# Softplus stages on a time line of the scan's half steps, in a four-layer hybrid kernel

## The chip, the core and the metric

The kernel runs on one NeuronCore of a Trainium2 chip. A core has TensorE (matmuls, into the memory PSUM), VectorE (elementwise work, reductions, scans), ScalarE (activation functions), GpSimd (here elementwise work, called POOL in the profile), and SyncE, whose queue (SP) issues nearly all DMAs. Each engine takes its own instructions strictly in the program's order; semaphores order them between engines. The metric is the device time of one launch in microseconds (us), lower is better.

## The reference

Four layers work on four images of 32 x 32 x 256. Layer 0 has a depthwise convolution and a state-space scan with 64 states for each of 512 channels, layer 1 a grouped convolution, layer 2 a masked attention and eight experts, layer 3 a scan with 16 states and eight experts. The change touches the step sizes of the two scans. In layer 0:

```python
proj = x @ w_x
dt_raw, Bm, Cm = jnp.split(proj, [R, R + N], axis=-1)
dt = jax.nn.softplus(dt_raw @ w_dt + dt_bias)
A = -jnp.exp(A_log)
def step(h, inp):
    xt, dtt, Bt, Ct = inp
    dA = jnp.exp(dtt[:, :, None] * A)
    h = dA * h + (dtt * xt)[:, :, None] * Bt[:, None, :]
    y = jnp.einsum('bdn,bn->bd', h, Ct)
    return (h, y)
```

and in layer 3 in the same way `dt = softplus(x_conv @ W_dt + b_dt)`, with a matrix of 512 x 512.

## The kernel before, in words

**The backbone.** `scans` runs eight scans one after the other, in the order (0,0), (0,1), (3,0), (0,2), (3,1), (0,3), (3,2), (3,3) of (layer, image): 256 units each for layer 0 and 64 for layer 3, 1280 in all. A unit is 128 rows of (state, channel) by 1024 time steps. A DMA loads dt, spread over the rows, into a tile `dA` (five buffers); ScalarE makes the exponential of it in place, in pairs of units; TensorE spreads dt*x to the rows (`ps_rep`, from the bf16 parts `S`, two buffers); VectorE multiplies by B and then runs the scan; GpSimd multiplies the result h by C; TensorE collects the rows (`ps_y`). The generator stops (`yield`) twice a unit, once after the multiply and once after the scan is issued: a half unit.

**The side chain.** All other work is one chain of stages (`STAGES`), issued between the half units: `front` 0 to 3 (layer 0 up to the step sizes of the image), `middle` b (the rest of layer 0 and all of layers 1 and 2, then `front3`, layer 3 up to the step sizes), `last` b (the rest of layer 3). A stage may start when its scan is done, or far enough. The scan of a later image needs the step sizes from a stage; `need` forces the chain on where they are not there in time. The last 64 units, (3,3), begin after `middle` 3; while the chain is at that, no scan is left to run beside it.

**How much of the chain goes between two half units.** `run` keeps a planned clock for each engine (`Metered`, fed with rough costs in us as instructions are issued). After each half unit it lifts every clock to at least 4 us (`LAG`) behind VectorE's, and then calls `advance`, which runs the chain to its next `yield`, up to twice (`TICKS`), as long as no clock is ahead of VectorE's:

```python
for e in clock:
    clock[e] = max(clock[e], now - LAG)
for _ in range(TICKS):
    if max(clock.values()) > clock["vector"] + LEAD or self.advance() is None:
        break
```

These clocks set the order of the program; nothing of them is known at run time.

**The softplus stage.** `steps` makes dt and dt*x of one image in eight items (d, g): four blocks of 128 channels by two halves of 512 time steps. For an item, `project` is the product in PSUM (`ps_dt`; one matmul in layer 0, four in layer 3), Relu to `r` and Abs to `e` on ScalarE (`linear`), then a load of the table for Exp and Ln, Exp, Identity with bias 1 and Ln to `l` (`soft`). `add` is one operation on VectorE (reads the PSUM tile) and three on GpSimd: dt ends up in `r`, dt*x in `l`. `split` issues the store of dt to DRAM (SP), casts dt*x to bf16 on ScalarE, has VectorE subtract that (`sp_x`), and casts the rest on ScalarE: the two upper of three bf16 parts. `low` makes the third on GpSimd, `store` issues the store of the three parts. Buffers: `r` and `l` three, `e` two, the parts three. `pipe` runs five steps as a software pipeline: one tick holds `store`, `low`, `split`, `add` and `project` of five items in sequence, the oldest first, and yields once.

For the last scan, (3,3), the first two items are done ahead of the rest, in another order (`between`), and `beside` puts a tick of another generator, the experts of image 2, behind each tick of this stage.

Of the kernel before, what the change touches and what calls it, by code (L numbers as in the profile page):

```python
# [31 lines left out]
SCANS = ((0, 0), (0, 1), (3, 0), (0, 2), (3, 1), (0, 3), (3, 2), (3, 3))  # L32
# [9 lines left out]
SCATTERED = 1  # L42
AHEAD = 12
LATEST = 5
DRAIN = 4
BETWEEN = 8

# [2 lines left out]
LEAD, LAG, TICKS = 0.0, 4.0, 2  # L50
# [87 lines left out]


END = object()  # L140


class Hybrid:
# [56 lines left out]
    def pipe(self, items, *steps, cost=1.0, cut=False):  # L200


        items = list(items)
        for tick in range(len(items) + len(steps) - 1):
            for s in reversed(range(len(steps))):
                if 0 <= tick - s < len(items):
                    steps[s](items[tick - s])
                    if cut and s:
                        yield cost
            yield cost if tick < len(items) else 0.5  # L210
# [173 lines left out]
    def scans(self, mp, psum):  # L384
# [15 lines left out]
        final = next(k for k, unit in enumerate(units) if unit[0] == SCANS[-1])  # L400
        units[final:final] = [None] * DRAIN
        final += DRAIN
        chunks, rows, waiting = {}, {}, []
# [60 lines left out]
        def chunks_ahead(k, late=False):  # L464
# [5 lines left out]
            while waiting:  # L470
                scan, d = units[waiting[0]][:2]
                if ("parts", *scan, d) not in self.ready:
                    if waiting[0] - k > (1 if waiting[0] == final else LATEST):
                        break
# [145 lines left out]
    def run(self):  # L620

        self.done, self.ready = set(), set()
        self.todo, self.stage, self.wait = list(STAGES), None, None
        self.alone, self.reached, self.passed = False, 0, set()
        nc, tc = self.nc, self.tc
        with tc.tile_pool(name="scan", bufs=1) as mp, tc.tile_pool(
            name="scps", bufs=1, space=PSUM
        ) as psum, tc.tile_pool(name="sdps", bufs=1, space=PSUM) as side, tc.manual_schedule():
            self.side_psum(side)
            self.scan_psum = psum  # L630
            self.mask_work, self.sorted = self.setup(), False
            clock = self.clock = dict.fromkeys(Metered.COST, 0.0)
            self.nc = Metered(nc, clock)
            for n, _ in enumerate(self.scans(mp, psum)):
                now = clock["vector"]
                if n % 2 and clock["gpsimd"] < now:
                    next(self.mask_work, None)
                for e in clock:
                    clock[e] = max(clock[e], now - LAG)
                for _ in range(TICKS):  # L640
                    if max(clock.values()) > clock["vector"] + LEAD or self.advance() is None:
                        break
            while self.advance() is not None:
                pass
            self.nc = nc
        assert not self.todo

    def steps(self, fp, key, w, src, chunks, bias, u, between=None):  # L650


        nc = self.nc
        for d in range(DC):
            self.keep(("dt", *key, d), [P, L])
            self.keep(("parts", *key, d), [3, P, L], BF16)
        got = {}

        def tile2(tag, bufs):
            return fp.tile([P, 512], F32, tag="sp_" + tag, name="sp_" + tag, bufs=bufs)  # L660

        def linear(item):
            d, g = item
            ps = self.ps("ps_dt")
            self.mm(ps, lambda k: w(k, d), src, chunks, slice(g * 512, (g + 1) * 512))

            r, e, l = (tile2(t, n) for t, n in (("r", 3), ("e", 2), ("l", 3)))
            nc.scalar.activation(r, ps, AF.Relu, bias=bias[:, d : d + 1])
            nc.scalar.activation(e, ps, AF.Abs, bias=bias[:, d : d + 1])
            got[item] = r, e, ps, l  # L670

        def soft(item):
            _, e, ps, l = got[item]
            nc.scalar.activation(e, e, AF.Exp, scale=-1.0)
            nc.scalar.activation(ps, e, AF.Identity, bias=1.0)
            nc.scalar.activation(l, ps, AF.Ln)

        def project(item):
            linear(item)
            self.log_table()  # L680
            soft(item)

        def add(item, by=nc.gpsimd):
            d, g = item
            r, e, one, l = got[item]
            nc.vector.scalar_tensor_tensor(e, one, -1.0, e, ALU.add, ALU.subtract)
            by.tensor_tensor(l, l, e, ALU.subtract)
            by.tensor_tensor(r, l, r, ALU.add)
            by.tensor_tensor(l, r, u[:, d, g * 512 : (g + 1) * 512], ALU.mult)

        def split(item):
            d, g = item
            r, _, _, x = got[item]
            nc.sync.dma_start(self.mem["dt", *key, d][:, g * 512 : (g + 1) * 512], r)
            X = fp.tile([P, 3, 512], BF16, tag="parts", name="parts", bufs=3)
            rest = tile2("x", 2)
            nc.scalar.copy(X[:, 0, :], x)
            nc.vector.tensor_tensor(rest, x, X[:, 0, :], ALU.subtract)
            nc.scalar.copy(X[:, 1, :], rest)
            got[item] = rest, X  # L700

        def low(item, by=nc.gpsimd):
            rest, X = got[item]
            by.tensor_tensor(X[:, 2, :], rest, X[:, 1, :], ALU.subtract)

        def store(item):
            d, g = item
            _, X = got.pop(item)
            nc.sync.dma_start(
                self.mem["parts", *key, d][:, :, g * 512 : (g + 1) * 512].rearrange("s p t -> p s t"), X  # L710
            )
            if g == 1:
                self.ready.add(("parts", *key, d))

        items = [(d, g) for d in range(DC) for g in range(2)]
        if between is not None:
            ahead, items = items[:2], items[2:]
            for item in ahead:
                linear(item)
            self.log_table()  # L720
            for item in ahead:
                soft(item)
            yield from between
            self.begin(key)
            for item in ahead:
                add(item, nc.vector)
            for item in ahead:
                split(item)
            self.two_loads()
            for item in ahead:  # L730
                low(item, nc.vector)
            self.first_parts = [got.pop(item)[1] for item in ahead]
            self.parts_direct(range(1), nc.scalar)
            self.ready.add(("parts", *key, 0))
            yield 3.0
        yield from self.pipe(items, project, add, split, low, store, cost=3.0)

# [871 lines left out]
    def moe(self, which, b, tb, side="right", pause=False):  # L1611
# [8 lines left out]
        with ExitStack() as stack:  # L1620
# [8 lines left out]
            def begin():  # L1629
                nonlocal op  # L1630
                op = stack.enter_context(tc.tile_pool(name=f"m{which}{b}", bufs=1, side=side))
                weights[0] = expert_weights(0)
# [68 lines left out]
            if pause:  # L1701
                yield END
                begin()
# [367 lines left out]
    def beside(self, main, other, begin=lambda: True):  # L2071

        held = None
        for cost in main:
# [3 lines left out]
            held = None  # L2078
            more = next(other, END)
            if more is END:  # L2080
                other = None
# [8 lines left out]
    def rest(self, other):  # L2090
        for more in other or ():
            if more is END:
                return
            yield more
# [14 lines left out]
    def last(self, b):  # L2109
# [4 lines left out]
        if b == NB - 1:  # L2114
            for more in self.other:
                if more is not END:
                    yield more
# [50 lines left out]
```

## Time and profile before

| | us |
|---|---|
| median of 3 runs (6305.61 to 6317.68) | 6310.74 |
| the profiled execution | 6294.21 |
| its span, from first to last instruction | 6292.5 |
| VectorE busy | 5032.7 (80%) |
| TensorE busy (matmuls) | 5142.7 (82%) |
| GpSimd busy | 3825.9 (61%) |
| ScalarE busy | 3410.6 (54%) |

The profile is one execution on the chip. In its lines an instruction is named by engine, operation and tiles, "out<-in"; buffer numbers are left out. `x` before a number is a count. A line of a group has the busy time, the mean in ns of one instruction, then the idle time of the engine just before the group's instructions and what ended most of it. A line of waits has the total of a kind, how often, and the longest. A line of windows has the stretch in us from the span's start and its length, then the busy time of each engine in it, the share of its full clock that TensorE was granted, the share of DMA time and GB/s. All source lines are L131, the helper that counts the planned clocks, so groups are told apart by their tiles: `sp_r`, `sp_e`, `sp_l`, `sp_x`, `parts` and `ps_dt` are the softplus stage's.

When softplus stages run (first activation to the end of the last third part), and how many scan units were started before each:

| scan | us | units |
|---|---|---|
| (0,0) | 94 to 216 | 0 to 19 |
| (0,1) | 409 to 515 | 61 to 84 |
| (0,2) | 695 to 792 | 127 to 147 |
| (0,3) | 956 to 1058 | 189 to 210 |
| (3,0) | 2006 to 2108 | 443 to 463 |
| (3,1) | 3064 to 3167 | 699 to 719 |
| (3,2) | 4433 to 4535 | 1027 to 1047 |
| (3,3) | 5647 to 5779 | 1216 to 1234 |

### The profile page before, as it was taken

To read this page: it belongs to the slowest core of one execution; us is meant where nothing else is said; L and a number is where in the kernel's file an instruction comes from. 1 tells how busy PE (TensorE), PEld (TensorE's weight loads), DVE (VectorE), ACT (ScalarE), POOL (GpSimd) and SP (SyncE) were. 2 spreads that over 40 slices of the span, in tenths; PEclk is the share of its full clock that TensorE was granted. 3 is DMA by queue.
4 is the path that set the end of the run, shared out by engine and by line. 5 is a ranking of instruction groups with operands and counts; after the bars stand their busy time and mean duration, and the time that the engine had idled before them with its cause. 6 is when DMAs were issued, how large, how long until landed. Compare 5 with 4: busy or idle time off the path is not lost. (4 is left out here: it accounts for less than half of the span.)

```text
span 6292.5 us, 59823 instructions
## 1 busy us (share of the span) xinstructions
PE 5142.7 (82%) x20249; PEld 2117.1 (34%) x20249; DVE 5032.7 (80%) x4016; ACT 3410.6 (54%) x4299; POOL 3825.9 (61%) x1948
## 2 busy tenths in 40 slices
PE   5676785579798568979869969989689779997999
PEld 2122120132253122234225522244145332543566
DVE  5888898988898998889889988899889982317811
ACT  3565655345496435558638735567547544336621
POOL 2787768665586766568767756577867752006600
PEclk7687785589798668979969979979779889999989
DMA  3555555544355656445455576345545761027611
GB/s 109 160 158 167 165 175 185 159 150 136 113 173 177 194 165 170 132 128 191 159 178 174 182 179 165 119 150 195 174 156 179 208 161 48 19 73 184 166 34 34
DMA packets 347915, 934.97 MB, mean 149 GB/s; under 512 B 37748, under 2 KB 120256, under 8 KB 345984
## 3 DMA queue, kind: packets, MB, share of 16 engines
q1 hardware_dynamic: 344880, 928.38, 48.7%
q0 software_dynamic: 2128, 2.13, 0.2%
q8 instruction: 165, 2.70, 0.2%
q14 instruction: 166, 1.36, 0.1%
q10 hardware_dynamic: 576, 0.39, 0.0%
HBM read 841.02 MB, written 92.37 MB: 148 GB/s over the span
## 5 line engine op out<-in xcount | busy, mean ns | idle before, releaser
L131 POOL TENSOR_TENSOR h<-h,rows 128x1024 f32<-128x1024 f32 x1280 | 3024.2, 2366 | 1740.4 <-DVE h L131 1529.3
L131 DVE TENSOR_TENSOR_SCAN h<-dA,ps_rep 128x1024 f32<-128x1024 f32 x1280 | 2924.3, 2285 | 182.2 <-ACT dA L131 53.6
L131 DVE TENSOR_TENSOR ps_rep<-ps_rep,rows 128x1024 f32<-128x1024 f32 x1280 | 1549.4, 1210 | 142.6 <-PE ps_rep L131 141.7
L131 PE MATMUL ps_rep<-S,spread_L_conv_A_log 96*128 96x512 bf16 x2048 | 752.8, 456 | 770.3 <-DVE h L131 722.4
L131 ACT ACTIVATE dA<-dA,A_L_conv_A_log 128x1024 f32<-128x1024 f32 x1024 | 1125.4, 1142 | 440.0 <-DMA dA<-dt 405.7
L131 PE MATMUL ps_y<-h,collect_L_conv_A_log 128*32 128x512 f32 x4096 | 704.4, 741 | 15.3 <-POOL h L131 15.3
L131 PE MATMUL ps_e<-we,h_m 128*128 128x256 f32 x3072 | 709.4, 383 | 8.3 <-ACT h_m L131 8.3
L131 PEld LDWEIGHTS <-spread_L_conv_A_log 96*128 96x128 bf16 x2048 | 159.7, 102 | 1558.0 <-DVE h L131 1246.4
L131 PEld LDWEIGHTS ps_e<-we,h_m 128*128 128x128 f32 x3072 | 583.3, 191 | 159.2 <-ACT h_m L131 31.0
L131 PE MATMUL ps_h<-xTm,we 128*128 128x512 f32 x1280 | 603.3, 607 | 4.6 <-DMA we<-in_L_ffn_W_dram 4.5
L131 ACT ACT_TABLE_LOAD x402 | 515.8, 1283 | 37.0 <-PE ps_h L131 15.5
L131 ACT ACTIVATE h_m<-ps_h,cols 128x512 f32<-128x512 f32 x384 | 257.5, 686 | 423.0 <-PE ps_h L131 421.0
L131 ACT ACTIVATE p<-ps_sc 128x512 f32<-128x512 f32 x404 | 219.3, 594 | 316.7 <-PE ps_sc L131 306.1
L131 ACT ACTIVATE dA<-dA,A_L_attn_A_log 128x1024 f32<-128x1024 f32 x256 | 282.8, 1143 | 141.4 <-DMA dA<-dt 122.8
L131 PEld LDWEIGHTS ps_h<-xTm,we 128*128 128x128 f32 x1280 | 242.2, 193 | 281.0 <-issue 211.5
L131 PE MATMUL ps_rep<-S,spread_L_attn_A_log 96*128 96x512 bf16 x512 | 176.8, 433 | 160.2 <-DVE h L131 138.6
L131 PE MATMUL ps_at<-p,v 128*32 128x512 f32 x1024 | 270.7, 608 | 0.2 <-ACT p L131 0.2
L131 PE MATMUL ps_at<-p,ones 128*32 128x512 f32 x1024 | 270.7, 608 | 0.0
L131 DVE SCALAR_TENSOR_TENSOR tb_rows<-ps_e,cw,tb_rows 128x256 f32<-128x256 f32 x128 | 55.7, 477 | 242.8 <-PE ps_e L131 242.7
L131 PE MATMUL ps_sc<-qT,kT 32*128 32x512 f32 x808 | 244.0, 654 | 4.6 <-ACT p L131 2.0
L131 PE MATMUL ps_cv<-pad,diag 128*128 128x512 f32 x504 | 230.5, 597 | 0.0
L131 PEld LDWEIGHTS ps_y<-h,collect_L_conv_A_log 128*32 128x32 f32 x4096 | 93.2, 118 | 339.7 <-issue 216.6
(347 smaller groups left out, 5475.6 us busy)
## 6 DMA issues: line engine op xcount, KB each, us to landing
dA<-dt SPq DMA_DIRECT2D x1280, 512.0 KB
we<-in_L_ffn_W_dram SPq DMA_DIRECT2D x64, 512.0 KB
parts<-parts SPq DMA_DIRECT2D x60, 384.0 KB
S<-parts SPq DMA_DIRECT2D x90, 256.0 KB
dt<-sp_r SPq DMA_DIRECT2D x64, 256.0 KB
y<-yo SPq DMA_DIRECT2D x128, 128.0 KB
y_back<-y SPq DMA_DIRECT2D x64, 256.0 KB
we<-in_L_ffn_w_dram SPq DMA_DIRECT2D x64, 256.0 KB
```

Of the source, the lines that this page charges most:

```text
L131: return got(*args, **kw)
```

## The change

For all scans but the first, `steps` no longer goes through `pipe`. `project` is cut in two, `half` (the first half of the product's matmuls; none where there is only one) and `rest` (the others, and the activations), and `split` in two, `cut` (the store of dt, the first cast, VectorE's subtract) and `second` (the second cast). The seven steps get a place each on a time line of slots: item n's step stands at slot `period * n + at`, with a period of 4 and places 0, 1, 6, 12, 13, 15, 16, and for (3,3)'s six remaining items a period of 2 and places 0, 1, 3, 6, 7, 8, 9. In a slot the older item's step comes first. Every slot yields a `Slot`, an empty one too, and `run` ends its inner loop at a `Slot`, so that at most one is run for each half unit. The gate on the clocks stays as it was.

```diff
+PACE = (4, (0, 1, 6, 12, 13, 15, 16))
+PACE_LAST = (2, (0, 1, 3, 6, 7, 8, 9))
...
+class Slot(float):
+    pass
...
                 for _ in range(TICKS):
-                    if max(clock.values()) > clock["vector"] + LEAD or self.advance() is None:
+                    if max(clock.values()) > clock["vector"] + LEAD:
+                        break
+                    cost = self.advance()
+                    if cost is None or isinstance(cost, Slot):
                         break
...
+        pace = None if key == SCANS[0] else PACE_LAST if key == SCANS[-1] else PACE
...
-        def linear(item):
+        def product(item, ps, ks):
             d, g = item
-            ps = self.ps("ps_dt")
-            self.mm(ps, lambda k: w(k, d), src, chunks, slice(g * 512, (g + 1) * 512))
+            for k in ks:
+                nc.tensor.matmul(
+                    ps, lhsT=w(k, d), rhs=src[:, k, g * 512 : (g + 1) * 512],
+                    start=(k == 0), stop=(k == chunks - 1),
+                )
+
+        def linear(item, ps=None):
+            d, g = item
+            done = 0 if ps is None else chunks // 2
+            ps = self.ps("ps_dt") if ps is None else ps
+            product(item, ps, range(done, chunks))
...
-        def split(item):
+        def cut(item):
...
             nc.vector.tensor_tensor(rest, x, X[:, 0, :], ALU.subtract)
+            got[item] = rest, X
+
+        def second(item):
+            rest, X = got[item]
             nc.scalar.copy(X[:, 1, :], rest)
-            got[item] = rest, X
+
+        def split(item):
+            cut(item)
+            second(item)
...
-        yield from self.pipe(items, project, add, split, low, store, cost=3.0)
+        if pace is None:
+            yield from self.pipe(items, project, add, split, low, store, cost=3.0)
+            return
+
+        def half(item):
+            ps = got[item] = self.ps("ps_dt")
+            product(item, ps, range(chunks // 2))
+
+        def rest(item):
+            linear(item, got.pop(item))
+            self.log_table()
+            soft(item)
+
+        steps, due = (half, rest, add, cut, second, low, store), {}
+        for n, item in enumerate(items):
+            for one, at in zip(steps, pace[1]):
+                due.setdefault(pace[0] * n + at, []).append((one, item))
+        for t in range(max(due) + 1):
+            for one, item in due.get(t, ()):
+                one(item)
+            yield Slot(1.0)
```

## The prediction

> **What bounds it now.** First the page's first rows: VectorE is busy 80% of the span, TensorE 82%, neither full, so the stages must be told apart. The costliest groups show VectorE's backbone, 1280 units of one multiply and one scan:
>
> ```profile
> L131 DVE TENSOR_TENSOR_SCAN h<-dA,ps_rep 128x1024 f32<-128x1024 f32 x1280 | 2924.3, 2285 | 182.2 <-ACT dA L131 53.6
> L131 DVE TENSOR_TENSOR ps_rep<-ps_rep,rows 128x1024 f32<-128x1024 f32 x1280 | 1549.4, 1210 | 142.6 <-PE ps_rep L131 141.7
> ```
>
> 1.21 + 2.29 and the pipeline's own gap make 3.57 us a unit wherever nothing else is in the way. Until 5228 us, where the first 1216 units are done, whatever delays VectorE delays the end. Then VectorE stands until (3,3)'s softplus, with TensorE at 95 to 100% in side work. Busy time by stretch, in this order: the softplus stages of (0,1), (0,2), (0,3), (3,0), (3,1), (3,2), then 5228 to 5648, then the softplus stage of (3,3):
>
> ```profile
> core 0: us, PE busy (x) PEld busy (x) DVE busy (x) ACT busy (x) POOL busy (x), PEclk, DMA share, GB/s
> 403.70:515.60 111.90, 62.48 (x168) 10.28 (x166) 100.44 (x64) 71.73 (x92) 102.26 (x61) 0.54 0.53 163
> 694.20:792.90 98.70, 53.77 (x141) 8.13 (x144) 90.68 (x58) 67.21 (x88) 90.43 (x54) 0.51 0.55 169
> 951.40:1058.30 106.90, 57.89 (x156) 9.42 (x154) 93.49 (x60) 70.21 (x91) 92.38 (x55) 0.55 0.52 160
> 1999.70:2109.20 109.50, 69.39 (x204) 21.65 (x206) 88.51 (x59) 70.11 (x90) 91.00 (x54) 0.76 0.46 148
> 3057.90:3167.30 109.40, 69.25 (x205) 21.47 (x206) 88.56 (x58) 70.08 (x90) 90.98 (x54) 0.76 0.45 148
> 4426.60:4536.10 109.50, 69.38 (x204) 21.65 (x206) 89.03 (x59) 70.12 (x90) 91.00 (x54) 0.76 0.47 149
> 5228.00:5648.00 420.00, 399.53 (x1713) 186.71 (x1710) 84.28 (x221) 147.49 (x205) 38.10 (x30) 0.95 0.13 39
> 5676.00:5780.00 104.00, 76.90 (x242) 35.94 (x243) 74.60 (x57) 70.46 (x86) 70.76 (x42) 0.87 0.62 159
> ```
>
> Length less VectorE's busy time is 11.5 + 8.0 + 13.4 + 21.0 + 20.8 + 20.5 = 95 us of idle VectorE in the six. Its waits in the fifth, (3,1):
>
> ```profile
> DVE sp_e L131 <- ACT sp_l L131: 8.5, 1, 8.5
> DVE sp_x L131 <- ACT parts L131: 8.0, 4, 3.6
> DVE h L131 <- ACT dA L131: 3.7, 2, 1.9
> ```
>
> All three are waits for ScalarE: an item's `add` stands in VectorE's queue one tick behind its `project`, `split`'s subtract right behind its own cast, and a whole tick's activations stand before the next exponentials of the scan.
>
> **The waits removed.** Over the six stages the kinds sum to: sp_e for the Ln 5.4 + 2.7 + 5.4 + 3 x 8.5 = 39; sp_x for the cast 4.4 + 4.4 + 6.6 + 8.0 + 8.0 + 7.5 = 39; scan for its exponential 11; about 6 is the pipeline's. In the new order `add` is 5 slots behind `rest`, 2.5 units or 8.9 us, while Relu to Ln with the table load takes 0.68 + 0.68 + 1.28 + 0.63 + 0.60 + 0.60 = 4.5 us: covered. `cut` is 6 slots behind `add` (three POOL operations of 1.27, so 3.8 us, before it); its cast waits for nothing and is queued behind no new activation: covered. Of 89 us I take 80; ends 45 (the first kind and a bit) and 89.
>
> No arithmetic is added or dropped: 64 table loads, 7 activations, 2 VectorE and 4 POOL operations an item stay. The subtract sp_x takes 0.69 to 2.3 us, mean 1.64, long beside a running POOL; it again falls beside POOL's product h. Taken at nothing; between 0.69 and 2.0 each, 48 of them give -45 to +17.
>
> **SP and ScalarE queues.** `cut` issues the dt store one slot before item n+3 reuses that r buffer (three buffers); before, they were a tick apart, three units. Such a store's last packet ends 4.1 to 4.9 us after issue when a dA load is ahead. SP passes it at the end of scan k-1; Relu comes after multiply, sp_x, second cast (1.3 + 2.0 + 0.6 = 3.9) and after `rest`'s product, about 5.9: covered by 1 us. The `parts` store comes one slot after `low` instead of a tick, so SP may stand for POOL with dA loads behind it; a load goes out four units before its use, against 3 us for 512 KB at the stages' 150 to 170 GB/s: covered for several us. Second cast waits for sp_x; behind it in ScalarE are `rest` and the next pair of exponentials: 0.62 + 4.5 + 1.14 = 6.2 us against two units, a multiply and sp_e, 9.1 us, until that scan. Slack 2.9 us, and only at every second item (exponentials go in pairs).
>
> **A rule against it.** The products are now in two halves with a multiply or scan between. The row of the L3 stages' ps_dt has 732 ns a record, 8 an item, at granted clock 0.76; the conv stages', of the same 512 columns, sparser and at 0.51 to 0.55, 992. The Trainium skill, TensorE: Matmul & The Clock Gate, section "Why this matters for your kernels", says that idle gaps over some 3 us put the clock back to half. By the first row nothing is lost. By the rule the 24 L3 items take 8 x 0.26 = 2.1 us longer each; that uses up the slack of 2.9 and, with the scan's own matmuls slower, perhaps 1 us of stall at 12 items: 12 us. I take 3, inside the 80.
>
> **The delay added.** `Slot` ends the side loop, so at most one slot runs per half unit: 7 x 4 + 17 = 45 slots, 22.5 units at least. The gate stays (no clock above VectorE's), and its POOL clock decides: per unit 2.42 against VectorE's 3.55, per item 4.95 against 1.49, so (4.95 - 1.49) / (3.55 - 2.42) = 3 units an item, not the 2 of the pace. These are the planner's figures and set order, not time. Stepping that rule by hand, the four items that the 4 us of LAG pays for come every 2 units, later ones every 3, and the last item still has its 16 slots behind it: 27 to 28 units. The old order by the same rule: 21 to 22; the trace has 20 to 23. So a stage ends 5.5 to 6 units later.
>
> After (0,1) to (0,3) and (3,0) the chain waits for scans anyway: 45 units idle to unit 256, 49 to unit 512. After (3,1) and (3,2) it doesn't: `last` 0 ends at unit 835, three after its successor may start; `last` 1 at 1163, eleven after. The end of a paced stage leaves POOL's clock 3.4 us lower, which hastens `back3` (POOL bound) by 3.4 / 1.13 = 3 units. So `middle` 3 is 6 to 12 units late at unit 1216. Its attention began at 1209: ten of its 64 steps ran beside scans, 54 alone at one per 2.81 us. All ten move behind: 10 x 2.81 = 28 us. Back come two waits of the scans there, TensorE having been slow at the start:
>
> ```profile
> 5203.30 1.23 DVE L131 TENSOR_TENSOR ps_rep<-ps_rep,rows 128x1024 f32<-128x1024 f32 x1 [4.83 <-PE ps_rep L131]
> 5211.52 1.23 DVE L131 TENSOR_TENSOR ps_rep<-ps_rep,rows 128x1024 f32<-128x1024 f32 x1 [4.57 <-PE ps_rep L131]
> ```
>
> 28 - 9.4 = +19, taken as +20; ends +5 (most of the delay made up) and +52 (12 units at the 4.35 us that a unit with side work takes).
>
> **The last stage.** Six paced items, a slot each half unit at most, one tick of the experts of image 2 between slots: twice as many ticks as before in this stage. VectorE waits 25 us there now, but TensorE is the bound from 5780 on (100%) and the sums end with it; it idles 27 of 104 us in the window. By the same stepping, the parts of d=1 aren't stored by unit 1227, and `need` forces the rest of them out at once: VectorE waits some 10 us, TensorE is fed. I take 12 of the 27 us as gained; ends -22 and +10.
>
> **Sum.** -80 + 20 - 12 = -72. The profiled execution took 6294.2 us (span 6292.5), so 6222; the median of the runs, 6310.7, is 16.5 higher and the waits are counted in the same way: 6239.
>
> **Rivals.**
> *The delay eats it.* 12 units at 4.35 us: -80 + 52 = -28, no gain at the end: 6283. For it: no slack behind (3,1) and (3,2). Against: alone, a step costs 2.81 instead of 3.75 us.
> *Slower: ScalarE late for the exponentials.* One more wait of Relu, for its products or for the dt store in the r buffer, pushes the scan's exponentials behind. It decides where Relu is over 2.9 us late: each us beyond stops VectorE at each of 48 items. 72 us are gone at 1.5 us beyond; at 2.5 it is -72 + 120 = +48: 6359. For it: the row of scan waiting for dA is there already, dt store and Relu are close (1 us). Against: half the items have their exponentials issued before `rest`.
> *The pace does nothing.* The gate, not the pace, sets three units an item, and old and new order run alike; only the delay is left: about 6311 to 6330. Against: the waits come from the order, whose distances change under any gate.
> *More.* sp_x falls beside an idle POOL: -45 beyond: 6194.
>
> **How the numbers follow.** Forecast 0.57, the delay 0.18, slower 0.12, nothing 0.07, more 0.06. Likeliest alone 6205 to 6275; to 8 in 10 with the rivals and the ends of the costs: 6190 to 6312. A change of 0.2% (12.6 us, the spread of the three runs) can be told: faster 0.78 (forecast, more, most of the delay), same 0.08, slower 0.14 (the slower rival, a little of nothing).
>
> **What would show it.** In each of the six stages the waits sp_e for sp_l and sp_x for parts under 3 us in sum, VectorE's idle time under 4 us a stage; stages of 26 to 28 units instead of 20 to 23; unit 1216 reached 75 to 90 us sooner, with attention of image 3 beginning within two units of it; from there to (3,3)'s softplus some 25 us longer. It is wrong if waits of h for dA or of sp_r for ps_dt grow instead, if sp_x's mean leaves 1.4 to 1.9 us, or if attention begins where it did.

## The result and the profile after

The changed kernel takes 6354.88 us (median of 5 runs, 6351.84 to 6359.43), the kernel before 6305.61 (5 runs, 6293.44 to 6317.68): **slower, 1.008 times, interval 1.0063 to 1.0097.** The profiled executions have spans of 6353.1 and 6292.5 us, 60.6 apart. Cut at the ends that the prediction used, the last scan of unit 1216 and (3,3)'s first Relu, first before:

```profile
5227.82 2.29 DVE L131 TENSOR_TENSOR_SCAN h<-dA,ps_rep 128x1024 f32<-128x1024 f32 x1 [0.39 <-ACT dA L131]
5647.31 0.69 ACT L131 ACTIVATE sp_r<-ps_dt,cols 128x512 f32<-128x512 f32 x1 [3.00 <-PE ps_dt L131]
```

and after:

```profile
5224.24 2.29 DVE L133 TENSOR_TENSOR_SCAN h<-dA,ps_rep 128x1024 f32<-128x1024 f32 x1
5677.24 0.69 ACT L133 ACTIVATE sp_r<-ps_dt,cols 128x512 f32<-128x512 f32 x1 [3.00 <-PE ps_dt L133]
```

| stretch (us) | before | after | difference | predicted |
|---|---|---|---|---|
| start to the end of scan 1216 | 5230.1 | 5226.5 | -3.6 | -80 - 9.4 |
| from there to (3,3)'s first Relu, the side chain alone | 417.2 | 450.7 | +33.5 | +28 |
| from there to the end | 645.1 | 675.9 | +30.8 | -12 |

The profiled execution of the kernel before was one of its faster ones (6294.2 us, with medians of 6301 to 6311), so by the medians, which are 49.3 us apart, the first row is nearer -15 than -3.6. The other two rows repeat to within 5 us in the kernels below that have the same order there, but for one (e3).

The windows of the changed kernel: the softplus stages of (0,1), (0,2), (0,3) and (3,1), then the chain alone, then (3,3)'s stage. The columns are those of the windows shown before.

```profile
408.40:590.10 181.70, 106.66 (x257) 15.00 (x256) 154.29 (x101) 91.53 (x110) 156.16 (x93) 0.54 0.50 161
744.60:872.40 127.80, 71.82 (x182) 10.28 (x180) 107.68 (x75) 74.86 (x95) 108.28 (x62) 0.51 0.53 170
1022.00:1141.40 119.40, 66.71 (x181) 10.04 (x180) 107.34 (x71) 75.09 (x95) 104.77 (x60) 0.54 0.50 166
3072.20:3191.50 119.30, 74.96 (x225) 20.34 (x223) 105.70 (x71) 73.89 (x94) 103.45 (x59) 0.70 0.49 161
5226.50:5677.20 450.70, 428.13 (x1825) 192.31 (x1826) 82.14 (x221) 154.76 (x209) 38.75 (x31) 0.93 0.12 36
5706.00:5859.00 153.00, 106.88 (x332) 55.28 (x332) 81.25 (x68) 86.09 (x101) 74.73 (x43) 0.83 0.44 112
```

The stage of (3,1) holds 27 units in 119.3 us where it held 21 in 109.4. Six plain units at 3.57 us added to the old stage make 130.8, so this stage itself gives 11.5 us. VectorE's idle time in it falls from 20.8 us to 13.6, and its subtracts take 10.4 us instead of 13.0. That holds for the three L3 stages; (0,3) gives 5.4 in the same reckoning; but (0,2) loses 7.7 and (0,1), 40 units now, loses 12.7. Their windows end with a wait of `ln_st`, the first VectorE instruction of the next stage, 7.6 and 19.1 us. Without these two the six stages give some 46 us of the 80. The waits of VectorE in (3,1)'s stage after:

```profile
DVE sp_x L133 <- ACT parts L133: 9.3, 4, 4.3
DVE h L133 <- ACT dA L133: 1.7, 1, 1.7
DVE sp_x L133 <- POOL h L133: 1.2, 1, 1.2
```

The wait of sp_e for the Ln is gone, as forecast. The wait of sp_x for the cast isn't; it is longer than the 8.0 of before. The same kinds of VectorE's waits over the whole backbone, up to 5240 us, first before:

```profile
DVE sp_e L131 <- ACT sp_l L131: 53.0, 8, 11.9
DVE sp_x L131 <- ACT parts L131: 43.7, 24, 3.9
DVE ln_st L131 <- DMA x<-in_x_dram: 9.2, 2, 8.3
DVE y_back L131 <- DMA y_back<-y: 8.8, 4, 4.8
```

and after:

```profile
DVE sp_x L133 <- ACT parts L133: 54.8, 29, 4.7
DVE ln_st L133 <- POOL pad L133: 19.1, 1, 19.1
DVE ln_st L133 <- DMA x<-in_x_dram: 15.4, 2, 7.8
DVE y_back L133 <- DMA y_back<-y: 15.0, 9, 3.4
DVE sp_e L133 <- ACT sp_l L133: 13.4, 2, 11.2
```

sp_e gives 39.6 us (13 of each total are (0,0)'s stage, which isn't paced). sp_x takes 11 more. `ln_st`, the norm statistics with which the next `front` stage begins, takes 25 more (the two waits just named), and `y_back`, VectorE's operation on a reloaded y in `middle`, 16 more (25.3 with two smaller rows of its kind, 8.8 before). The subtracts, 17 us shorter in all, are the last of the larger terms: -39.6 + 11 + 25 + 16.5 - 17 is -4, as the first stretch shows. So the saving is there, and most of it comes back as other waits of the same engine.

**Why sp_x still waits.** The timeline of the changed kernel; a bracket holds the idle time before an instruction and what ended it. ScalarE:

```profile
3091.60 0.60 ACT L133 ACTIVATE sp_l<-ps_dt 128x512 f32<-128x512 f32 x1
3092.09 2.18 ACT L133 ACTIVATE dA<-dA,A_L_conv_A_log 128x1024 f32<-128x1024 f32 x2
3094.17 0.61 ACT L133 CAST parts<-sp_l 128x512 bf16<-128x512 f32 x1
...
3112.16 0.69 ACT L133 ACTIVATE sp_r<-ps_dt,cols 128x512 f32<-128x512 f32 x1 [6.47 <-DMA dt<-sp_r]
...
3118.60 0.60 ACT L133 CAST parts<-sp_l 128x512 bf16<-128x512 f32 x1
```

and VectorE:

```profile
3094.81 1.04 DVE L133 TENSOR_TENSOR sp_x<-sp_l,parts 128x512 f32<-128x512 f32 x1 [4.34 <-ACT parts L133]
...
3119.31 1.57 DVE L133 TENSOR_TENSOR sp_x<-sp_l,parts 128x512 f32<-128x512 f32 x1 [3.53 <-ACT parts L133]
```

The cast at 3094.17 has had its operand for 9.7 us (GpSimd's product ended at 3084.4); it stands behind the six instructions of a later item's `rest` and a pair of exponentials, and VectorE, with the subtract next in its own queue, stands 4.34 us for it. Eighteen us later Relu has waited 6.47 us for a dt store to leave the r buffer that it reuses, what is behind it on ScalarE is late with it, and again VectorE stands. The store of that dt is not slow, it is issued late:

```profile
3107.20 1.15 POOL L133 TENSOR_TENSOR parts<-sp_x,parts 128x512 bf16<-128x512 f32 x1
3108.38 0.39 SPq L736 DMA_DIRECT2D parts<-parts  x1
3108.82 0.48 SPq L714 DMA_DIRECT2D dt<-sp_r  x1
```

In the slot in which an item's dt store is issued, the `parts` store of the item before it comes first, and SP stands at that until GpSimd has made the third part. Such waits of Relu, none before, are 15 now:

```profile
ACT sp_r L133 <- DMA dt<-sp_r: 71.7, 15, 6.6
```

In all 15 the dt store follows the `parts` store directly, this one goes out as GpSimd's third part ends, and Relu starts 2.9 to 3.5 us after the dt store's issue.

**The last stretch.** TensorE in the 193 us from (3,3)'s first Relu on. Its window and its waits before:

```profile
5647.30:5840.30 193.00, 156.89 (x523) 76.89 (x522) 139.59 (x112) 131.47 (x153) 111.93 (x61) 0.91 0.69 183
PE ps_rep L131 <- DVE h L131: 16.1, 8, 3.7
PE ps_dt L131 <- ACT h_m L131: 6.6, 3, 2.8
```

and after:

```profile
5677.20:5870.20 193.00, 137.48 (x412) 68.47 (x411) 100.18 (x86) 112.09 (x134) 79.44 (x45) 0.85 0.50 130
PE ps_dt L133 <- ACT h_m L133: 13.0, 2, 7.1
PE ps_dt L133 <- DVE tb_rows L133: 9.3, 1, 9.3
PE ps_dt L133 <- DVE sp_e L133: 8.3, 2, 4.8
```

What ended these waits are readers of PSUM tiles: the experts' activation `h_m`, their sum `tb_rows`, an item's own `add`. The product waits for a free PSUM buffer, 30.6 us instead of 6.6, and everything behind it in TensorE's queue waits too. `half` takes one of the three slots of a rotation that the experts share and `add` gives it back three slots later, each with a tick of the experts behind it. TensorE idles 55.5 us of the 193 instead of 36.1.

So there were three places to test: what the last stage loses, what the delay costs, and what takes back the saving in the backbone. All ratios below are to the kernel before, run on the same chip at the same time.

### The profile page after: what moved, and what is told of

Its sections match the earlier page's. It is cut to its first block, busy times and chain, and to the rows that moved or that the text cites. A ratio compares the mean times of both kernels' runs of the same rounds, so it can differ in the third digit from the quotient of the medians.

```text
span 6353.1 us, 59852 instructions
## 1 busy us (share of the span) xinstructions
PE 5181.0 (82%) x20249; PEld 2115.6 (33%) x20249; DVE 5011.5 (79%) x4016; ACT 3412.5 (54%) x4296; POOL 3822.4 (60%) x1948
## 5 line engine op out<-in xcount | busy, mean ns | idle before, releaser
L133 PE MATMUL ps_y<-h,collect_L_conv_A_log 128*32 128x512 f32 x4096 | 733.1, 747 | 38.0 <-POOL h L133 38.0
```

Of the source, the lines that this page charges most:

```text
L133: return got(*args, **kw)
```

## The experiments

**1. The last stage, and the delay.** Three kernels with the change in some of the stages only:

```diff
-        pace = None if key == SCANS[0] else PACE_LAST if key == SCANS[-1] else PACE
+        pace = None if key in (SCANS[0], SCANS[-1]) else PACE                          # e1
+        pace = PACE_LAST if key == SCANS[-1] else None                                 # e2
+        pace = PACE if key in ((0, 1), (0, 2), (0, 3), (3, 0)) else None               # e3
```

> The change everywhere but in the last softplus stage, (3,3), which goes through the old pipe. Theory: of the 60 us lost between the two profiles, some 31 come from that stage (first Relu of (3,3) to the end: 645 us before, 676 after), because the product's first half takes a PSUM buffer that the experts share and holds it for about three half units longer; with the old pipe that stretch is again 645 us (within 6) and the whole about 30 us shorter than with the change: 6325, or 1.003 of before. Rival (the stretch is long only because the stage begins late, behind the delayed chain): the stretch stays at 670 or more and the time at 6345 or more.

> The change in the last softplus stage alone; the six stages beside scans keep the old pipe. Theory: first Relu of (3,3) at about 5647 us in the profile as before, from there to the end 676 us in place of 645: 31 us slower than before, 6337, ratio 1.005. Rival (the loss there follows from the late start, not from the pace): within 10 us of before.

> The pace in (0,1), (0,2), (0,3) and (3,0) only, where the side chain waits for scans behind the stage; the old pipe in (3,1), (3,2) and (3,3). Theory: no step of attention of image 3 moves behind the scans and the last stage is as before, so neither the 30 us of the stretch from unit 1216 to (3,3) nor the 31 us behind it are lost; of what the four stages save (sp_e waiting for the Ln, 22 us; sp_x shorter, about 11) the waits behind them take back most: 6290 to 6306, ratio 0.998 to 1.000. Rival (the loss is in the four paced stages, by what they push into the stages behind them): 6320 or more.

| | scan 1216 ends | chain alone | last stretch | ratio |
|---|---|---|---|---|
| before | 5230.1 | 417.2 | 645.1 | 1 |
| the change | 5226.5 | 450.7 | 675.9 | 1.008 (1.0063 to 1.0097) |
| e1, last stage piped | 5230.3 | 452.6 | 645.4 | 1.0041 (1.0025 to 1.0058) |
| e2, last stage alone paced | 5234.3 | 415.2 | 675.4 | 1.0053 (1.0033 to 1.0073) |
| e3, four stages with slack | 5243.6 | 418.5 | 652.4 | 1.0012 (1.0004 to 1.002) |

e1 and e2 agree to 0.6 us with the expected 645 and 676: the 31 us belong to the pace in the last stage, and not to its late start. e1 and e3 together show that the 33 us of the middle stretch belong to the pace in (3,1) and (3,2). e3 also shows that the four stages with slack behind them, the best case for the change, gain nothing: 1.0012, slightly outside the expected 0.998 to 1.000, 6311.62 us where the rival wanted 6320 or more. Its last stretch is 7 us longer than that of the other kernels with the old pipe there; the section on the hardware comes back to it. The rest of the account is in the backbone.

**2. What in the last stage costs it.** e7 keeps the number of slots and shortens the hold of the PSUM buffer from three slots to one; the two halves of a product stand in one slot again, too:

```diff
-PACE_LAST = (2, (0, 1, 3, 6, 7, 8, 9))
+PACE_LAST = (2, (1, 1, 2, 6, 7, 8, 9))
```

> The change, with the last stage's places 1, 1, 2 in place of 0, 1, 3 for half, rest and add, so that an item holds its PSUM buffer for one slot and not for three; all else, the number of slots too, is the change's. Theory (the 31 us of the last stretch come from TensorE standing behind a product that waits for a PSUM buffer): first Relu of (3,3) to the end falls from 676 to 645 to 655, the time to 6325 to 6335. Rival (they come from the stage taking more half units, with a tick of the experts between its slots): 670 to 680, the time as with the change.

Measured: last stretch 652.7 us, ratio 1.0036 (1.0024 to 1.0049). 23 of the 31 us go with the hold. TensorE's waits in the same 193 us of e7:

```profile
PE ps_h L133 <- ACT h_m L133: 14.7, 3, 7.4
...
PE ps_dt L133 <- DVE sp_e L133: 3.0, 2, 2.1
PE ps_dt L133 <- ACT h_m L133: 1.5, 1, 1.5
```

The wait of ps_dt falls from 30.6 us to 4.5, which speaks for the hold and not for the cut. What is left of the last stretch, 7.6 us, is as much as TensorE idles more (67.1 us over the whole stretch instead of 59.5), and shows as the experts' own wait for a buffer (ps_h, 14.7); which part of the time line makes it wasn't tried.

The clock goes the same way: in the second 100 us from (3,3)'s first Relu TensorE was granted 0.97 before, 0.87 with the change and 0.90 in e7. In these traces it is granted either the full clock or half of it, and of the 193 us it had the half for 34 before, 58 with the change and 38 in e7. With the change this stage has five waits of ps_dt between 3.5 and 9.3 us; before, the longest gap in the second 100 us is 2.8 us. That agrees with the rule that the prediction weighed elsewhere (the Trainium skill, TensorE: Matmul & The Clock Gate, "Why this matters for your kernels": gaps over some 3 us put the clock back to half). Its share is the smaller one: TensorE worked 38 us at half clock instead of 28, which costs 5 us (an estimate), while its idle time grew by 19.

**3. The size of the delay.** e8 leaves the break at a slot out, so that two slots may go between half units again:

```diff
-                    if cost is None or isinstance(cost, Slot):
+                    if cost is None:
```

> The change without the break: up to two slots between half units, as before the change. In the program's order the last middle stage then stands 4 units later than before the change, in place of 8. Theory of the delay: unit 1216 to (3,3)'s first Relu takes 430 to 437 us (417 before, 451 with the change), the last stretch 676 as with the change. The waits of VectorE beside the six stages: sp_e for sp_l stays under 15 us, since five places lie between the Ln and add still; unit 1216 within 12 us of the change's. Time 6335 to 6345. Rival (what counts is the one slot for each half unit): sp_e's wait comes back to over 30 us and unit 1216 is 15 us or more later.

e6 lifts GpSimd's planned clock at the end of a paced stage. This delays the chain more, and takes away the credit on which the next stage starts:

```diff
             yield Slot(1.0)
+        self.clock["gpsimd"] = max(self.clock.values())
```

> The change, with the planned clock of GpSimd lifted to the highest clock at the end of each paced stage, so that the next stage of the side chain starts without credit; in the program's order the last middle stage then stands 12 units later than before the change, in place of 8. Theory of the delay: the stretch from unit 1216 to (3,3)'s first Relu, 417 us before and 451 with the change (30 to 33 us for 8 units), grows to 462 or more (3.7 to 4.2 us for each of the 4 further units). Theory of the credit (a paced stage leaves GpSimd's planned clock 4 us behind, so the next stage's steps are issued faster than their loads land: ln_st 25 us of new waits, y_back 16): ln_st waits under 10 us in all, y_back under 8, and unit 1216 is reached 15 to 35 us sooner than with the change. Together 6335 to 6355. Rival: ln_st and y_back wait as long as with the change (the loads are late for another reason), then unit 1216 is where the change has it and the end near 6365.

In the program's order, the `middle` 3 stage's norm (b0st) stands behind this many units, and this many of attention's score products (ps_sc) run before the last scan of (3,2):

| | units | score products | chain alone (us) |
|---|---|---|---|
| before | 1173 | 68 | 417.2 |
| e8 | 1177 | 36 | 430.0 |
| the change | 1181 | 0 | 450.7 |
| e6 | 1185 | 0 | 451.5 |

Up to 8 units the delay has the expected price (e8: 430.0 in the forecast of 430 to 437). The 462 for 12 units was wrong, and the column of score products says why: with the change all of attention is already behind the scans, and there is nothing more to push out. The price of the delay is the attention that it moves, and ends there.

Otherwise e8 went the rival's way in part: unit 1216 came 16.7 us later than with the change, by the medians some 10 less. sp_e's wait stayed away (15 us), but VectorE's wait for the exponentials is 72 us instead of 45, and ps_rep's 168 instead of 137 (up to 5200 us). Two slots in one half unit put more of ScalarE's and TensorE's side work ahead of what the next scan needs. That the one slot for each half unit is worth something is likely by these waits, but not shown by the time.

**4. The next stage's start.** e6 for its other theory: VectorE's waits up to 5240 us.

```profile
DVE ln_st L133 <- DMA x<-in_x_dram: 19.0, 3, 10.2
DVE y_back L133 <- DMA y_back<-y: 8.5, 6, 3.4
```

ln_st waits 24 us instead of 40 (its row of the program's start, 5 us, in both), so the fall is smaller than forecast; y_back 8.5 instead of 25, close to the forecast of under 8. Scan 1216 ends at 5199.4, 27 us sooner than with the change. Some 14 of these lie in units 512 to 699, where no softplus stage runs and where these kernels take between 776 and 796 us in the profiles; so the profiles alone give 13 to 27. The ratio is 1.0038 (1.0024 to 1.0052) against the change's 1.008, so about half of what the change loses goes, though nothing was done to its order within a stage. A paced stage yields once each half unit and lets GpSimd's planned clock fall behind; the following stage is then issued as fast as the loop allows. Behind (0,1) and (0,2) its first ln_st stands three units after the stage's last subtract, with e6's line five. With the change, behind (0,1):

```profile
578.68 1.15 POOL L133 TENSOR_TENSOR parts<-sp_x,parts 128x512 bf16<-128x512 f32 x1 [4.60 <-issue]
579.86 0.38 SPq L736 DMA_DIRECT2D parts<-parts  x1
582.87 0.37 SPq L834 DMA_DIRECT2D x<-in_x_dram  x1
588.99 0.43 DVE L133 BATCH_NORM_STATS2 ln_st<-x 128x6 f32<-128x256 f32 x1 [19.14 <-POOL pad L133]
```

SP stands at the stage's last `parts` store until GpSimd has made the third part, the load of x comes behind that store, and VectorE, with ln_st next in its queue, waits for the load (the profile names POOL, but ln_st reads x). Here GpSimd's work on the attention's mask, which runs beside the first scans, lies in between as well; behind (0,2), without it, the same chain costs 7.6 us. Two of y_back's waits, 8.6 us together, come 460 us after the last paced stage beside scans; how the credit leads to these was not traced.

**5. The cast.** e4 moves the dt store alone, three slots up; e5 also moves the first cast and the subtract one slot down, ahead of a later item's activations in the same slot:

```diff
-            r, _, _, x = got[item]
-            nc.sync.dma_start(self.mem["dt", *key, d][:, g * 512 : (g + 1) * 512], r)
+            x = got[item][3]
...
+        def early(item):
+            d, g = item
+            r = got[item][0]
+            nc.sync.dma_start(self.mem["dt", *key, d][:, g * 512 : (g + 1) * 512], r)
...
-        steps, due = (half, rest, add, cut, second, low, store), {}
+        steps, due = (half, rest, add, early, cut, second, low, store), {}
...
-PACE = (4, (0, 1, 6, 12, 13, 15, 16))
+PACE = (4, (0, 1, 6, 9, 12, 13, 15, 16))          # e4
+PACE = (4, (0, 1, 6, 9, 13, 14, 15, 16))          # e5
```

> The change, with the dt store three slots sooner (place 9 in place of 12) and the first cast and its subtract one slot later, in the same slot as the activations of a later item but ahead of them (places 13 and 14); the last stage is as in the change. Theory (sp_x waits because its cast stands in ScalarE's queue behind a later item's activations, which wait for the r buffer until dt is stored): sp_x waiting for parts falls from 55 us over the six stages to under 15, and sp_r waiting for the dt store from 6 to 11 us a stage to under 2; unit 1216 is reached 30 to 45 us sooner than with the change, and the end some 35 us sooner: 6320. Rival (what one wait gives the next takes, since ScalarE and GpSimd are near full in these stages): unit 1216 less than 15 us sooner, and other waits of VectorE (h for dA, sp_e for sp_l) grow by as much.

> The change with one thing alone of two tried together earlier: the dt store stands at place 9 in place of 12, the casts stay where the change has them. Together the two took VectorE's wait of sp_x for the cast from 55 us to 18 up to unit 1216. Theory A (the cast is late because the activations ahead of it on ScalarE wait for the r buffer): this alone takes sp_r's wait for the dt store from 72 us to under 10 and sp_x's wait to under 30. Theory B (the cast is late by the activations and exponentials themselves, which stand ahead of it): sp_r's wait goes, but sp_x's wait stays at 40 or more. Under A unit 1216 is some 10 us sooner than with the change, under B within 8 us of it; the rest of the time is as with the change: 6335 to 6355.

| up to 5200 us (us) | the change | e4 | e5 |
|---|---|---|---|
| sp_r waits for the dt store | 71.7 | 0 | 0 |
| sp_r waits for ps_dt | 45.7 | 109.2 | 146.0 |
| sp_x waits for the cast | 54.8 | 31.7 | 18.1 |
| scan waits for dA | 44.5 | 65.9 | 56.7 |
| multiply waits for ps_rep | 137.2 | 142.7 | 147.5 |
| scan 1216 ends | 5226.5 | 5216.7 | 5212.3 |

e4, waits of VectorE up to 5240 us:

```profile
DVE h L133 <- ACT dA L133: 65.9, 70, 3.8
DVE sp_x L133 <- ACT parts L133: 31.7, 23, 4.3
```

and e5:

```profile
DVE h L133 <- ACT dA L133: 56.7, 73, 3.4
DVE sp_x L133 <- ACT parts L133: 18.1, 10, 4.7
```

Both causes are real: the store's hold of the r buffer made 23 us of the wait, the place behind the activations 14 (e4's place 9 puts the dt store ahead of the `parts` store at which SP stood). But the backbone got only 10 and 14 us shorter where e5 was to give 30 to 45, which is the rival's "less than 15"; of e4's 10, 9 lie in units 512 to 699, beside no softplus stage, of e5's 14 none: sp_r now waits for its product instead of for the store, and the exponentials, which share ScalarE with these activations, are later by 12 to 21 us. e5's ratio is 1.0064 (1.0047 to 1.0081), e4's 1.007 (1.005 to 1.009); against the change's 1.008 the runs can't tell either from it, and the waits are the evidence.

**6. Putting it together.** e9 has e5's order in (0,2), (0,3) and (3,0) alone, where a delay is free and no mask work runs, and the old pipe elsewhere. e10 adds e6's line. e11 and e12 add (3,1) and (3,2) on shorter time lines, without the break and the lift:

```diff
-        pace = None if key == SCANS[0] else PACE_LAST if key == SCANS[-1] else PACE
+        pace = PACE if key in ((0, 2), (0, 3), (3, 0)) else None                       # e9, e10
+        pace = PACE if key in ((0, 2), (0, 3), (3, 0)) else PACE_LAST if key in ((3, 1), (3, 2)) else None
...
+PACE_LAST = (2, (0, 0, 2, 4, 5, 5, 6, 6))                                              # e11
+PACE_LAST = (3, (0, 1, 4, 7, 10, 11, 11, 12))                                          # e12
```

> The pace, with the dt store sooner and the first cast ahead of a later item's activations, in (0,2), (0,3) and (3,0) only; the old pipe, from the kernel before, in all other stages. Behind these three the side chain waits for scans, and no mask work stands beside them. Theory (a paced stage saves some 10 to 16 us where cast and store are not held up, and its delay is free there): no delay at unit 1216 (stretch 417 us, last stretch 645), unit 1216 reached 20 to 35 us sooner than before: 6270 to 6285, ratio 0.995 to 0.998. Rival (the stages' gain is given back by the stages behind them, whose loads are then late): ratio 0.999 to 1.002.

> The kernel with the new order in (0,2), (0,3) and (3,0) alone, which ran at 0.9986 of before, with GpSimd's planned clock lifted at the end of each of the three. Theory (their loads come late because the next stage starts on credit): ln_st's wait falls from 15 us to under 12 and y_back's from 19 to under 8, and the time by 10 to 15 us: 6283 to 6290, ratio 0.9965 to 0.9975. Rival (nothing is to be had there): within 0.0006 of 0.9986.

> As e10_three_no_credit, and in (3,1) and (3,2) a short time line without the break: period 2, places 0, 0, 2, 4, 5, 5, 6, 6, so that the two casts stand in a slot of their own between the activations of two items; in the program's order no later stage moves. Theory (a wait is avoided where the cast isn't behind fresh activations, and nothing is lost where the chain isn't delayed): stretch from unit 1216 to (3,3) 417 us, sp_x's wait 4 to 7 us less in each of the two stages, sp_e's unchanged: 8 to 14 us under e10_three_no_credit. Rival (the distance of two slots, not the order in a slot, makes the waits): no difference beyond 5 us.

> As e10_three_no_credit, and in (3,1) and (3,2) a time line of period 3, places 0, 1, 4, 7, 10, 11, 11, 12, without the break; in the program's order the last middle stage stands 3 units later than before. Theory: the stretch from unit 1216 to (3,3) grows from 417 by some 3 x 3.3 = 10 us to 425 to 430, and the two stages give 10 to 16 us each: 10 to 22 us under e10_three_no_credit. Rival (stages this short bring the waits back): no faster than it.

| | scan 1216 ends | chain alone | last stretch | time (us) | ratio |
|---|---|---|---|---|---|
| e9 | 5236.8 | 415.3 | 644.9 | 6297.96 | 0.9986 (0.9979 to 0.9994) |
| e10 | 5223.9 | 417.2 | 646.6 | 6285.06 | 0.9974 (0.9967 to 0.9982) |
| e11 | 5218.7 | 415.3 | 644.5 | 6281.59 | 0.9969 (0.996 to 0.9978) |
| e12 | 5209.5 | 424.0 | 645.3 | 6279.73 | 0.9963 (0.995 to 0.9975) |

e9 is the first kernel faster than before, by less than expected (0.995 to 0.998). Its scans end 7 us later in the profile, 9 of these in units 512 to 699; by the medians, 6297.96 against 6307.94 for the kernel before, and with the other two stretches as before, its backbone is some 8 us shorter. e10's ratio lies in the forecast of 0.9965 to 0.9975, but the gain over e9 is 0.0012, some 8 us and not the expected 10 to 15, and the two intervals overlap; its y_back wait fell only from 23 to 16.5 us, not under 8. e11's and e12's forecasts were too high: 3.5 and 5.3 us by the medians, and their intervals overlap e10's. In e11 sp_x's wait over the backbone is 27.7 us against e10's 29.4, so its rival holds: at a distance of two slots the order within a slot did next to nothing. In e12 the chain alone takes 7 us longer for 3 units, a little less than the 8 to 13 expected, and the backbone gives 14. All of e10 to e12 beat the kernel before, by 0.26 to 0.37%; which of them is the fastest the intervals leave open.

## Why the prediction was wrong

- **"sp_e for the Ln ... 39": right.** 53.0 to 13.4 us, 39.6.
- **"`cut` is 6 slots behind `add` ...; its cast waits for nothing and is queued behind no new activation: covered": wrong, the first failed step.** 39 us were to go, and 11 were added. The prediction measured the distance from the cast's operand to the cast, and not what lies ahead of the cast on ScalarE: `rest` of a later item is three slots ahead, and with its product's wait, its 4.5 us and a pair of exponentials it isn't done in time. The second half of the same error is **"covered by 1 us"** for the dt store: sp_r waited 71.7 us for it. The store took less than the 4.1 to 4.9 us reckoned; what failed is "SP passes it at the end of scan k-1", as SP stood at the `parts` store ahead of it for GpSimd. The prediction saw that "SP may stand for POOL", but counted the dA loads behind and not the dt store. e4 and e5 show the two shares, 23 and 14 us. The third kind, 11 us of scans waiting for their exponentials, mostly stayed (46.8 to 44.5 us over the backbone).
- **What the freed time meets next: missing from the sum.** The prediction had seen that a paced stage "leaves POOL's clock 3.4 us lower", and counted it as a help to `back3`. The same credit issues the next stage ahead of its loads: ln_st and y_back took back 42 us, and e6 gave 13 to 27 of it back with one line. With sp_x's 50 us off the forecast this is why scan 1216 came 3.6 us sooner, 15 by the medians, and not the 75 to 90 forecast.
- **"sp_x taken at nothing, -45 to +17": inside.** Its busy time fell by 17 us over the six stages; the median of one went from 2.00 to 1.50 us.
- **The clock gate: right to cost it at little.** ps_dt in the L3 stages has a median of 593 ns in both profiles, granted 0.70 after and 0.76 before: the products did not become slower by being cut.
- **"ten of its 64 steps ... 28 us": right in kind, the size near.** All of attention moved behind the scans, 8 units late, in the forecast's 6 to 12; the stretch grew by 33.5. The "two waits of the scans there", 9.4 us, did go (in units 1152 to 1216 ps_rep waits 12 us less), but the whole term was booked at 20 and stood at 33 where it could be read.
- **"TensorE is fed. I take 12 of the 27 us as gained": wrong in sign, 31 us lost.** The prediction counted how many ticks of the experts go into the stage, and not what the product holds in the meantime. `need` did force the last items out, at unit 1228, as said, but VectorE waited 26 us there and not some 10, and TensorE was not fed: at least 9.4 of the 30.6 us for a PSUM buffer fall into that forced run, the others before it. Most of the loss is by the buffer held for three slots (e7: 23 of 31).
- **The rivals.** The slower one, ScalarE late for the scans' exponentials, gave 6359, near the measured 6355, by chance: Relu did wait for the dt store, but what came late behind it was the cast, and the scans' wait for dA was 44.5 us after and 46.8 before. That part of its mechanism showed only in e4, e5 and e8. The delay was the second rival, and real, but one part of three.

By the profiles the three stretches give -4, +33 and +31; the forecast for them was -89, +28 and -12. The first and the last are the ones that failed.

## What to carry to other kernels

Work out a wait at the place where the awaited instruction stands in its own engine's queue, with everything ahead of it, and not from when its operand is ready: a step with operands ready for 10 us can be late. When a step is cut in two and spread over time, list what it holds between the halves (a PSUM slot, a buffer whose store must land first) and who else rotates through it. A stage that becomes slower or smoother changes the start of the stage behind it; a saving is one only when it is still there at the next point where all engines meet, and where the delayed chain has no slack, its price is the work that is pushed behind that point, and no more.

## What the runs showed of the hardware that was not expected

The same stretch of program isn't equally steady everywhere. The last stretch repeated to about 2 us in six of the seven kernels that have the old pipe there (645.1, 645.4, 644.9, 646.6, 644.5, 645.3), while units 512 to 699, with no softplus stage in them, took 776 to 796 us in the profiles: a difference of 10 us in one profiled part of the backbone isn't a finding by itself. The seventh is e3, with 652.4. Its first 193 us from (3,3)'s first Relu:

```profile
5662.10:5855.10 193.00, 155.91 (x495) 76.64 (x494) 131.67 (x107) 124.60 (x146) 106.69 (x59) 0.87 0.68 178
```

TensorE idles 37.1 us there where it was 36.1 before, but it was granted 0.87 instead of 0.91: it had the half clock for 51 us instead of 34, and worked at it for 44 instead of 28. The difference at half speed is 8 us, an estimate, of the 7 measured. Two of its gaps are 5.10 and 4.65 us where before they are 3.03 and 1.49. So two gaps that were a little longer seem to have cost more by the clock than by their length, in the direction of the rule named above; a kernel made to show this alone was not run.

And the same subtract on 128x512 took from 0.68 to 2.24 us within one kernel. It took 0.69 us in the eight places where GpSimd was idle beside it, and 1.50 in the mean where GpSimd was busy. Moving it, with no wait removed, took 17 us off the busy time of 48 of them.
